# Paired transfers of edge features and receivers, and an even stream of single-row loads, in a graph-network kernel

## The chip, the cores and the metric

The kernel runs on one core of one Trainium2 chip. The metric is the device time of one execution in microseconds. Times are the median of several executions; a profile is one more execution, recorded by the hardware profiler.

## The reference

One message-passing layer over a graph of 6250 nodes and 206250 edges, sorted by receiver, followed by a residual and a layer norm. In the code below `senders` is `src`, `receivers` is `dst`, and the two feature arrays have 32 columns each; D is 128, with 8 heads of 16.

```python
w_ij = silu(edge_feats @ rad_W1 + rad_b1) @ rad_W2 + rad_b2
w_ij = w_ij + (silu(chi_scalar @ sph_W1 + sph_b1) @ sph_W2 + sph_b2)
q_i = (node_feats @ Wq)[receivers]            # by heads
k_j = (node_feats @ Wk)[senders]
alpha = (q_i * w_ij * k_j).sum(axis=-1) / sqrt(HEAD_DIM) * cutoffs[:, None]
v_j = (node_feats @ Wv)[senders]
out = segment_sum(alpha[..., None] * v_j, receivers, num_segments=n_nodes) / 16.0
x = layernorm(x + out)
```

## The kernel before

**Tiles, quads and groups.** 128 edges are a tile, four tiles a quad, and four quads a group; there are 403 quads in 101 groups (NG). The main loop goes over groups and, in each, over four slots, one quad a slot, in the order 0, 2, 1, 3. `i` counts slots.

**Before the loop** the keys and values of all nodes are computed and written to a table in DRAM, `kv_tab`, one row of 1 KB a node. The receivers of each edge, relative to the quad's first node, are turned so that a tile's 128 numbers lie in one row (`relT`), written to DRAM (`rel_lin`, L481), and copied from there four times over into `rel_four` (L486), from which a group's receivers can be read as one broadcast.

**A slot of the loop** works on several quads in different stages. TensorE runs the first layers of quad i+2 (L560), brings the queries of quad i+1 to its edges (`q_at_edges`, L579), runs the second layers of quad i+1 (`weigh`, L612), and sums the messages of the group before (L664). ScalarE applies SiLU to quad i+2 (L597). VectorE multiplies the queries of quad i+1 by its keys (`multiply`, L628), then multiplies quad i by the second layers' output (L636), reduces (L638), scales (L641) and forms the messages (L653). The last product of `q_at_edges` is the slot's mark: ScalarE's SiLU, VectorE's multiply, GpSimd's next gathers and some of SyncE's loads wait for it.

**Keys and values** come in two ways. GpSimd gathers one tile of 128 rows per instruction from `kv_tab` (L141), 14 slots ahead, four instructions a quad. For 60 of the quads, spread evenly between slots 8 and 401 (`row_at`, six or seven slots apart), the fourth tile is not gathered. Its 128 rows are fetched by 128 single DMAs of 1 KB (L214) into a tile `wide`: 60 issued from SyncE's queue (SP), 68 from ScalarE's. The row addresses are read from `at_i` into registers by loads (L208), two for SyncE's share of a tile and three for ScalarE's. `multiply` waits for a row tile's semaphore (L625).

**How the rows are dealt.** `load_rows(i)` ends each slot's code. It knows one row tile at a time. Tile k is dealt from slot `row_at[k-1] - 4` to slot `row_at[k] - 5`; in each of these slots each queue is owed an equal part of the tile's units, where a row is one unit and a load of registers is ROW_LOAD = 5. `next_rows` issues what is owed. ScalarE keeps ROW_CARRY = 2 units back, which are issued between the next slot's SiLUs. `wide` has three buffers.

**SyncE's queue** runs in program order and also issues, once a group: the node rows `x` (L315), the features of group g+3 (`load_feats`, L252, 512 KB, three buffers), the receivers of group g+3 (`load_rel`, L263, 128 KB, four buffers), and the write of finished rows (L773). The loads of `x` and of the features wait for a mark of TensorE.

Of the kernel before, what the change touches and what calls it, by code (L numbers as in the profile page):

```python
# [12 lines left out]
F32 = mybir.dt.float32  # L13
BF16 = mybir.dt.bfloat16
U8 = mybir.dt.uint8
# [6 lines left out]
SP = mybir.EngineType.SP  # L22
ACT = mybir.EngineType.Activation
WAIT = mybir.DependencyInfo(mybir.DependencyClass.Sync, mybir.DependencyReason.DATA)

P = 128
# [6 lines left out]
GT = 16  # L33
QT = 4
NQ = GT // QT
NG = math.ceil(E / (P * GT))
NT = NG * GT
EG = P * GT
EQ = P * QT
QUADS = math.ceil(E / EQ)  # L40
NB = math.ceil(N / P)
NBC = 7
ROWS = (NB + 1) * P
W = 32
LB = 4
ROW_BYTES = 2 * D * 4
# [4 lines left out]
ROW_TILES = 60  # L51
ROW_FIRST = 8
ROW_LAST = 401
ROW_LEAD = 5
ROW_ACT = 68
ROW_AT = {SP: 0, ACT: 64}
ROW_LOAD = 5
ROW_CARRY = 2
ROW_UNITS = {SP: 32, ACT: 24}
XU = 4  # L60
# [3 lines left out]
ROW_SEMS = 8  # L64
# [8 lines left out]
def gnn_kernel(ctx, tc, x, src, dst, weight, edges, rad_W1, rad_b1, rad_W2, rad_b2,  # L73
# [14 lines left out]
    nc = tc.nc  # L88
    const = ctx.enter_context(tc.tile_pool(name="const", bufs=1))
    dram = ctx.enter_context(tc.tile_pool(name="dram", bufs=1, space=DRAM))  # L90

    kv_tab = dram.tile([NB * P, 2 * D], F32, name="kv_tab")
    rel_lin = dram.tile([NT, P], BF16, name="rel_lin")
    rel_four = dram.tile([NT // QT, NQ, EQ], BF16, name="rel_four")
    acc = dram.tile([ROWS, D], F32, name="acc")

    wkv = const.tile([P, 2 * D], F32, name="wkv")
# [39 lines left out]
    def quad_of(name, bufs, width=D):  # L137
        return ep.tile([P, QT, width], F32, name=name, bufs=bufs)
# [11 lines left out]
    row_of = {}  # L150
    row_done = {}
    rows_left = {SP: [], ACT: []}
    owed = {SP: 0, ACT: 0}
    row_work = {}
    row_issued = {}
    row_sems = [tc.alloc_semaphore(f"rows_{n}") for n in range(ROW_SEMS)]
    row_count = [0] * ROW_SEMS
# [4 lines left out]
    def next_rows(engine, n, loads=True):  # L162

        left = rows_left[engine]
        n = min(n, owed[engine])
        while n > 0 and left and (loads or left[0][0] == 1):
            cost, issue = left.pop(0)
            issue()
            n -= cost
            owed[engine] -= cost  # L170
# [19 lines left out]
        kv_of[q] = kv  # L190
        kv_done[q] = kv_sems[at], kv_count[at]

    def load_rows(i):

        k = next((k for k in range(ROW_TILES) if i <= row_at[k] - ROW_LEAD), None)
        start = None if k is None else (row_at[k - 1] if k else ROW_FIRST) - ROW_LEAD + 1
        if k is None or i < start:
            return next_rows(ACT, owed[ACT])
        q = order[row_at[k]]
        slots = row_at[k] - ROW_LEAD + 1 - start  # L200
        table = kv_tab.bitcast(U8).rearrange("(o n) b -> o (n b)", o=1)

        def rows_by(engine, name, a, b):
            regs = {}

            def load(e, m):
                c = ROW_AT[name] + e - a
                regs.update(zip(range(e, e + m), nc.values_load_multi_w_load_instructions(  # L208
                    at_i[k:k + 1, c:c + m], engines=(name,), min_val=0,
                    max_val=(N - 1) * ROW_BYTES,  # L210
                    skip_runtime_bounds_check_because="senders are nodes")[1]))

            def row(p):
                signalled(engine.dma_start(row_of[q][p:p + 1, 0, :].bitcast(U8),  # L214
                                           table[:, ds(regs.pop(p), ROW_BYTES)]))

            items = []
            for e in range(a, b, ROW_UNITS[name]):
                m = min(ROW_UNITS[name], b - e)
                items.append((ROW_LOAD, lambda e=e, m=m: load(e, m)))  # L220
                items += [(1, lambda p=p: row(p)) for p in range(e, e + m)]
            rows_left[name] += items
            return sum(cost for cost, _ in items)

        def signalled(o):
            tc.no_tile_sem_insts.add(o.ins.name)
            tc.add_to_no_dep_group(f"rows_{q}", o.ins)
            o.then_inc(row_sems[k % ROW_SEMS], 16)
            row_count[k % ROW_SEMS] += 16
            row_done[q] = row_sems[k % ROW_SEMS], row_count[k % ROW_SEMS]  # L230
            row_issued[q] = row_issued.get(q, 0) + 1

        n = P - ROW_ACT
        if i == start:
            row_of[q] = quad_of("wide", 3, P)[:, :2, :].rearrange("p t d -> p (t d)")[:, None, :]
            row_work[SP] = rows_by(nc.sync, SP, 0, n)
            row_work[ACT] = rows_by(nc.scalar, ACT, n, P)
        for engine, m in row_work.items():
            a, b = (math.ceil(m * j / slots) for j in (i - start, i - start + 1))
            owed[engine] += b - a  # L240
        next_rows(SP, owed[SP])
        next_rows(ACT, owed[ACT] - ROW_CARRY)

    def kv_parts(q, t):

# [1 line left out]
            return [(t, kv_of[q][:, t, :])]  # L247
        return [(slice(0, QT - 1), kv_of[q][:, :QT - 1, :]), (slice(QT - 1, QT), row_of[q])]

    def load_feats(g, mark=None):  # L250
        feats_of[g] = gp.tile([P, EG // 2], F32, name="feats", bufs=3)
        o = nc.sync.dma_start(feats_of[g], edges[g])  # L252
        if mark is not None:
            tc.add_manual_dep(o.ins, mark.ins.name, WAIT, reason="one signal of TensorE a quad")

    def quads_in(g):
        return min(NQ, QUADS - g * NQ)

    def load_rel(g, pool, bufs):

        relb_of[g] = pool.tile([P, EQ], BF16, name="relb", bufs=bufs)
        r = rel_four[g * NQ:(g + 1) * NQ].rearrange("j n e -> (j n) e")
        nc.sync.dma_start(relb_of[g], r[:, None, :].to_broadcast([NQ * NQ, W // NQ, EQ]))  # L263

    made = []

# [72 lines left out]
    with tc.tile_pool(name="nodes", bufs=1) as nodes, \  # L339
# [134 lines left out]
            nc.tensor.transpose(pt[:n, 0, :], rel[:, t:t + n], ident)  # L474
            nc.scalar.activation(relT[:n, t // P, :], pt[:n, 0, :], AF.Copy)

        def store_rel(a, b):
            for i, n in ((slice(a, min(b, NT // P)), P), (slice(NT // P, b), NT % P)):
                if i.start < i.stop:
                    t = slice(i.start * P, i.start * P + (i.stop - i.start) * n)  # L480
                    nc.sync.dma_start(rel_lin[t, :].rearrange("(n p) e -> p n e", p=n), relT[:n, i, :])  # L481
            a, b = a * P // QT, min(b * P, NT) // QT
            r = rel_lin.rearrange("(q t) e -> q (t e)", t=QT)
            for a, b in ((a, b - b % (P // 8)), (b - b % (P // 8), b)):
                if a < b:
                    nc.sync.dma_start(rel_four[a:b], r[a:b, None, :].to_broadcast([b - a, NQ, EQ]))  # L486

        def first_rel():
            turn_rel(0)
# [29 lines left out]
        for i, (k, n) in enumerate(work):  # L519
# [20 lines left out]
            if i == len(chunks) - 1:  # L540
                load_rel(0, gp, 1)
                load_feats(0)
                for g in range(1, XL):
                    load_x(g)
                    load_feats(g)
                nc.sync.dma_start(scale, weight)
        for q in order[XQ:AHEAD]:
            gathers(q)
        nc.vector.tensor_tensor(bsum, b2[:, 0:1], b2[:, 1:2], op=OP.add)
        store_rel(1, math.ceil(NT / P))  # L550
        nc.vector.tensor_scalar(scale, scale, SCALE, None, op0=OP.mult)


    with tc.tile_pool(name="ps", bufs=1, space=PSUM) as pp, tc.tile_pool(name="loop", bufs=1) as lp:
# [241 lines left out]
            nc.vector.tensor_scalar(general, found, 0.0, None, op0=OP.is_gt)  # L796

        written, ready, ready_at = [], [], []
        load_rel(1, lp, 4)
        load_rel(2, lp, 4)  # L800
        silus(order[0], first_layers(order[0]))
        pick(1)
        q_at_edges(order[0])
# [4 lines left out]
        for g in range(NG - 1):  # L808
            for slot, j in enumerate((0, 2, 1, 3)):
# [34 lines left out]
                if slot == 0:  # L844
                    if g + XL < NG:
                        load_x(g + XL, past)
                if slot == 3 and g + 3 < NG:
                    load_feats(g + 3, past)
                if slot == 2 and g + 3 < NG:
                    load_rel(g + 3, lp, 4)  # L850
                if slot == 0 and 1 <= g:
                    one_hots(g)
                if slot == 1:
# [254 lines left out]
```

## Time and profile before

| | |
|---|---|
| median of 3 executions | 2596.52 us (2588.82 to 2597.5) |
| the profiled execution | 2599.59 us, its span 2597.7 us |
| mean granted TensorE clock | 0.837 |
| busy: PE, PEld, DVE, ACT, POOL | 2090.8, 1744.9, 1525.9, 645.0, 1470.8 us |
| gathers on GpSimd (L141) | 1520, 945 ns each |
| single rows from SyncE / from ScalarE (L214) | 3600 / 4080 |
| features, receivers (L252, L263) | 101 x 512 KB, 101 x 128 KB |

PE is TensorE's matmul, PEld its weight load, DVE is VectorE, ACT ScalarE, POOL GpSimd, SP SyncE; a q behind the name means the engine's sequencer, which waits and issues DMAs. A line of a group of instructions gives line, engine, operation, output and inputs, count, busy time, mean ns of one, then the idle time before them and what ended most of it. "Remote" stands where the profile cannot name what ended a wait. A line of the waits gives who waited for whom, microseconds in total, times, and the longest. A row of the timeline gives start, duration, instruction and count, then the idle time before it. For one line's instructions the three durations are minimum, median and maximum in ns.

### The profile page before, as it was taken

To read this page: it belongs to the slowest core of one execution; us is meant where nothing else is said; L and a number is where in the kernel's file an instruction comes from. 1 tells how busy PE (TensorE), PEld (TensorE's weight loads), DVE (VectorE), ACT (ScalarE), POOL (GpSimd) and SP (SyncE) were. 2 spreads that over 40 slices of the span, in tenths; PEclk is the share of its full clock that TensorE was granted. 3 is DMA by queue.
4 is the path that set the end of the run, shared out by engine and by line. 5 is a ranking of instruction groups with operands and counts; after the bars stand their busy time and mean duration, and the time that the engine had idled before them with its cause. 6 is when DMAs were issued, how large, how long until landed. Compare 5 with 4: busy or idle time off the path is not lost.

```text
span 2597.7 us, 56700 instructions
## 1 busy us (share of the span) xinstructions
PE 2090.8 (80%) x15990; PEld 1744.9 (67%) x15990; DVE 1525.9 (59%) x3427; ACT 645.0 (25%) x1359; POOL 1470.8 (57%) x1564
## 2 busy tenths in 40 slices
PE   5678888888888788878888878888887888888787
PEld 4567677666767666666667667666766767676666
DVE  3456556656656555656656556555656556565567
ACT  1122222222222222222222222222222222222223
POOL 4456565655565565555556555555555555565540
PEclk7788888888888888888888797888788787887888
DMA  5543444434343343434434434444343343443331
GB/s 180 173 118 112 120 124 116 121 112 122 113 123 116 116 124 114 120 112 122 121 111 123 119 114 121 115 120 121 114 120 118 111 122 115 119 124 108 118 103 35
DMA packets 157219, 307.18 MB, mean 118 GB/s; under 512 B 42022, under 2 KB 91360, under 8 KB 156896
## 3 DMA queue, kind: packets, MB, share of 16 engines
q0 software_dynamic: 73984, 201.43, 27.2%
q1 hardware_dynamic: 72976, 97.35, 11.4%
q10 hardware_dynamic: 9936, 4.72, 0.8%
q8 instruction: 127, 2.08, 0.3%
q14 instruction: 196, 1.61, 0.2%
HBM read 289.88 MB, written 15.11 MB: 117 GB/s over the span
## 4 chain that ended last, share of the span: by engine, by line
PE 38%; issue 20%; SPq 13%; DVE 13%; another core or an unknown queue 10%; ACTq 5%; ACT 1%; DMA 0%; DVEq 0%
PE pw L612 17%; SPq L214 10%; PE pq L579 7%; PE ph L560 6%; ACTq L214 4%; PE po L664 3%; DVE kq L628 3%; DVE side L638 2%; DVE kq L636 2%; SPq L208 2%; PE pq L705 1%; ACT act L597 1%; PE pk L381 1%; PE pq L286 1%
## 5 line engine op out<-in xcount | busy, mean ns | idle before, releaser
L141 POOL DMA_INDIRECT kv<-kv_tab,src_i x1520 | 1436.9, 945 | 1042.9 <-remote 447.9
L612 PE MATMUL pw<-w,act 128*128 128x128 f32 x6448 | 1060.4, 324 | 109.1 <-issue 107.6
L612 PEld LDWEIGHTS pw<-w,act 128*128 128x128 f32 x6448 | 951.7, 231 | 187.0 <-issue 149.7
L597 ACT ACTIVATE act<-ph,b 128x512 f32<-128x512 f32 x806 | 554.7, 689 | 1843.5 <-remote 1374.7
L628 DVE TENSOR_TENSOR kq<-pq,kv 128x512 f32<-128x512 f32 (+1 forms) x404 | 270.6, 670 | 931.3 <-remote 680.0
L560 PE MATMUL ph<-feats,w 32*128 32x512 f32 x1612 | 665.7, 740 | 138.5 <-issue 128.8
L579 PE MATMUL pq<-q,hotT 32*128 32x128 f32 x3224 | 557.5, 321 | 20.9 <-issue 17.8
L579 PEld LDWEIGHTS pq<-q,hotT 32*128 32x128 f32 x3224 | 470.7, 220 | 33.0 <-issue 32.7
L560 PEld LDWEIGHTS ph<-feats,w 32*128 32x128 f32 x1612 | 190.7, 207 | 303.6 <-issue 272.0
L638 DVE TENSOR_REDUCE side<-kq 128x32 f32<-128x512 f32 x404 | 280.2, 694 | 14.0
L653 DVE TENSOR_TENSOR msg<-kv,side 128x512 f32<-128x512 f32 (+1 forms) x404 | 268.7, 665 | 13.9
L636 DVE TENSOR_TENSOR kq<-pw,kq 128x512 f32<-128x512 f32 x404 | 274.1, 679 | 0.0
L664 PE MATMUL po<-msg,hot 128*32 128x128 f32 x3200 | 183.2, 309 | 34.2 <-issue 34.1
L567 PE MATMUL pw<-brow,onesb 3*128 3x512 bf16 x403 | 176.5, 438 | 0.0
L664 PEld LDWEIGHTS po<-msg,hot 128*32 128x32 f32 x3200 | 84.5, 118 | 91.2 <-issue 63.6
L705 PE MATMUL pq<-part,to 128*128 128x128 f32 x196 | 56.6, 380 | 107.6 <-issue 54.4
L705 PEld LDWEIGHTS pq<-part,to 128*128 128x128 f32 x196 | 38.6, 245 | 122.2 <-issue 83.7
L641 DVE TENSOR_TENSOR side<-side,scale 128x32 f32<-128x32 f32 x400 | 79.7, 199 | 13.7
L381 PE MATMUL pk<-wkv,xT 128*128 128x256 f32 x162 | 45.6, 424 | 38.0 <-DVE kv L382 23.9
L292 DVE TENSOR_TENSOR hotT<-relb,side 128x512 f32<-128x512 bf16 x101 | 68.6, 679 | 0.0
L286 PE MATMUL pq<-wq,xT 128*128 128x128 f32 x200 | 49.6, 336 | 23.5 <-issue 15.9
L382 DVE COPY kv<-pk 128x512 f32<-128x512 f32 (+1 forms) x41 | 27.4, 682 | 68.9 <-remote 48.5
(126 smaller groups left out, 892.9 us busy)
## 6 DMA issues: line engine op xcount, KB each, us to landing
wide<-kv_tab ACTq DMA_DIRECT2D x4080, 1.0 KB
wide<-kv_tab SPq DMA_DIRECT2D x3600, 1.0 KB
feats<-in_edges SPq DMA_DIRECT2D x101, 512.0 KB
kv<-kv_tab,src_i POOLq DMA_INDIRECT x1520, 2.9
relb<-rel_four SPq DMA_DIRECT2D x101, 128.0 KB
x<-in_x SPq DMA_DIRECT2D x101, 64.0 KB
out<-y SPq DMA_DIRECT2D x101, 64.0 KB
kv_tab<-kv SPq DMA_DIRECT2D x12, 512.0 KB
```

The lines of the kernel that those rows point to most:

```text
L141: return nc.gpsimd.indirect_dma_start(out=o, out_offset=None, in_=table, in_offset=bass.IndirectOffsetOnAxis(ap=index, axis=0))
L214: signalled(engine.dma_start(row_of[q][p:p + 1, 0, :].bitcast(U8), table[:, ds(regs.pop(p), ROW_BYTES)]))
L560: return nc.tensor.matmul(act_of[q, i], w1[r0:r0 + R, :], feats_of[g][r0:r0 + R, c0:c0 + EQ], start=True, stop=True)
L567: nc.tensor.matmul(pw, onesb[f:f + 3, :], brow[f:f + 3].rearrange("p t d -> p (t d)"), start=True, stop=False)
L579: o = nc.tensor.matmul(pq_of[q][:, t, :], hotT_of[g][b, t * P:(t + 1) * P], q_of[g][b, :], start=True, stop=True)
L597: o = nc.scalar.activation(act, act_of[q, i], AF.Silu, bias=b1[:, i:i + 1])
L612: o = nc.tensor.matmul(pw[:, t, :], act_of[q, i][:, t * P:(t + 1) * P], w2[:, i, :], start=False, stop=(t == QT - 1 and i == 1))
L628: o = nc.vector.tensor_tensor(kq_of[q][:, u, :], pq_of[q][:, u, :], kv[:, :, :D], op=OP.mult)
L636: nc.vector.tensor_tensor(m, pw_of[q][:, t, :], m, op=OP.mult)
L638: nc.vector.tensor_reduce(alpha, m.rearrange("p t (h e) -> p t h e", e=HD), AX.X, OP.add)
L653: nc.vector.tensor_tensor(msg_of[q][:, u, :].rearrange("p t (h e) -> p t h e", e=HD), kv[:, :, D:].rearrange("p t (h e) -> p t h e", e=HD) ...
L664: o = nc.tensor.matmul(po_of[g][j * W:(j + 1) * W, :], hot_of[g][:, j * QT + t, :], msg_of[g * NQ + j][:, t, :], start=(t == 0), stop=(t = ...
```

## The change

Features and receivers are loaded for two groups at a time: `load_feats` and `load_rel` take a pair u (groups 2u and 2u+1), are called in the odd groups only, and keep two buffers of double size each. For this the receivers lie in DRAM by pairs (`rel_pair`), and `store_rel` writes them with more and smaller DMAs: ten writes and six broadcasts in all, where there were three and three. The row tiles are no longer dealt one at a time. `load_rows(i)` works out how many tiles are due by slot i as one number, 60/393 of a tile a slot; it opens each tile as this number passes it, and owes each queue the units between the last slot's number and this one's. A load of registers now counts six units, and the lead is six slots.

```diff
--- before.py
+++ after.py
@@ -38,6 +38,7 @@
 EG = P * GT
 EQ = P * QT
 QUADS = math.ceil(E / EQ)
+PAIRS = math.ceil(NG / 2)
 NB = math.ceil(N / P)
 NBC = 7
 ROWS = (NB + 1) * P
@@ -51,10 +52,10 @@
 ROW_TILES = 60
 ROW_FIRST = 8
 ROW_LAST = 401
-ROW_LEAD = 5
+ROW_LEAD = 6
 ROW_ACT = 68
 ROW_AT = {SP: 0, ACT: 64}
-ROW_LOAD = 5
+ROW_LOAD = 6
 ROW_CARRY = 2
 ROW_UNITS = {SP: 32, ACT: 24}
 XU = 4
@@ -90,8 +91,8 @@
     dram = ctx.enter_context(tc.tile_pool(name="dram", bufs=1, space=DRAM))
 
     kv_tab = dram.tile([NB * P, 2 * D], F32, name="kv_tab")
-    rel_lin = dram.tile([NT, P], BF16, name="rel_lin")
-    rel_four = dram.tile([NT // QT, NQ, EQ], BF16, name="rel_four")
+    rel_lin = dram.tile([2, PAIRS, GT, P], BF16, name="rel_lin")
+    rel_pair = dram.tile([PAIRS, NQ, NQ, 2, EQ], BF16, name="rel_pair")
     acc = dram.tile([ROWS, D], F32, name="acc")
 
     wkv = const.tile([P, 2 * D], F32, name="wkv")
@@ -151,7 +152,8 @@
     row_done = {}
     rows_left = {SP: [], ACT: []}
     owed = {SP: 0, ACT: 0}
-    row_work = {}
+    row_dealt = {SP: 0, ACT: 0}
+    row_open = []
     row_issued = {}
     row_sems = [tc.alloc_semaphore(f"rows_{n}") for n in range(ROW_SEMS)]
     row_count = [0] * ROW_SEMS
@@ -190,15 +192,11 @@
         kv_of[q] = kv
         kv_done[q] = kv_sems[at], kv_count[at]
 
-    def load_rows(i):
-
-        k = next((k for k in range(ROW_TILES) if i <= row_at[k] - ROW_LEAD), None)
-        start = None if k is None else (row_at[k - 1] if k else ROW_FIRST) - ROW_LEAD + 1
-        if k is None or i < start:
-            return next_rows(ACT, owed[ACT])
+    def open_tile(k):
+
         q = order[row_at[k]]
-        slots = row_at[k] - ROW_LEAD + 1 - start
         table = kv_tab.bitcast(U8).rearrange("(o n) b -> o (n b)", o=1)
+        row_of[q] = quad_of("wide", 3, P)[:, :2, :].rearrange("p t d -> p (t d)")[:, None, :]
 
         def rows_by(engine, name, a, b):
             regs = {}
@@ -211,8 +209,14 @@
                     skip_runtime_bounds_check_because="senders are nodes")[1]))
 
             def row(p):
-                signalled(engine.dma_start(row_of[q][p:p + 1, 0, :].bitcast(U8),
-                                           table[:, ds(regs.pop(p), ROW_BYTES)]))
+                o = engine.dma_start(row_of[q][p:p + 1, 0, :].bitcast(U8),
+                                     table[:, ds(regs.pop(p), ROW_BYTES)])
+                tc.no_tile_sem_insts.add(o.ins.name)
+                tc.add_to_no_dep_group(f"rows_{q}", o.ins)
+                o.then_inc(row_sems[k % ROW_SEMS], 16)
+                row_count[k % ROW_SEMS] += 16
+                row_done[q] = row_sems[k % ROW_SEMS], row_count[k % ROW_SEMS]
+                row_issued[q] = row_issued.get(q, 0) + 1
 
             items = []
             for e in range(a, b, ROW_UNITS[name]):
@@ -222,24 +226,20 @@
             rows_left[name] += items
             return sum(cost for cost, _ in items)
 
-        def signalled(o):
-            tc.no_tile_sem_insts.add(o.ins.name)
-            tc.add_to_no_dep_group(f"rows_{q}", o.ins)
-            o.then_inc(row_sems[k % ROW_SEMS], 16)
-            row_count[k % ROW_SEMS] += 16
-            row_done[q] = row_sems[k % ROW_SEMS], row_count[k % ROW_SEMS]
-            row_issued[q] = row_issued.get(q, 0) + 1
-
         n = P - ROW_ACT
-        if i == start:
-            row_of[q] = quad_of("wide", 3, P)[:, :2, :].rearrange("p t d -> p (t d)")[:, None, :]
-            row_work[SP] = rows_by(nc.sync, SP, 0, n)
-            row_work[ACT] = rows_by(nc.scalar, ACT, n, P)
-        for engine, m in row_work.items():
-            a, b = (math.ceil(m * j / slots) for j in (i - start, i - start + 1))
-            owed[engine] += b - a
+        row_open.append({SP: rows_by(nc.sync, SP, 0, n), ACT: rows_by(nc.scalar, ACT, n, P)})
+
+    def load_rows(i):
+
+        tiles = min(max((i - ROW_FIRST + ROW_LEAD) * ROW_TILES / (ROW_LAST - ROW_FIRST), 0), ROW_TILES)
+        while len(row_open) < math.ceil(tiles):
+            open_tile(len(row_open))
+        for engine in owed:
+            due = sum(min(max(tiles - k, 0), 1) * work[engine] for k, work in enumerate(row_open))
+            owed[engine] += math.ceil(due) - row_dealt[engine]
+            row_dealt[engine] = math.ceil(due)
         next_rows(SP, owed[SP])
-        next_rows(ACT, owed[ACT] - ROW_CARRY)
+        next_rows(ACT, owed[ACT] - (ROW_CARRY if tiles < ROW_TILES else 0))
 
     def kv_parts(q, t):
 
@@ -247,20 +247,31 @@
             return [(t, kv_of[q][:, t, :])]
         return [(slice(0, QT - 1), kv_of[q][:, :QT - 1, :]), (slice(QT - 1, QT), row_of[q])]
 
-    def load_feats(g, mark=None):
-        feats_of[g] = gp.tile([P, EG // 2], F32, name="feats", bufs=3)
-        o = nc.sync.dma_start(feats_of[g], edges[g])
+    def pair_of(u):
+        return range(2 * u, min(2 * u + 2, NG))
+
+    def load_feats(u, mark=None):
+        pair = pair_of(u)
+        feats = gp.tile([P, 2, EG // 2], F32, name="feats")
+        for g in pair:
+            feats_of[g] = feats[:, g - pair[0], :]
+        o = nc.sync.dma_start(feats[:, :len(pair), :],
+                              edges[pair[0]:pair[-1] + 1].rearrange("g p e -> p g e"))
         if mark is not None:
             tc.add_manual_dep(o.ins, mark.ins.name, WAIT, reason="one signal of TensorE a quad")
 
     def quads_in(g):
         return min(NQ, QUADS - g * NQ)
 
-    def load_rel(g, pool, bufs):
-
-        relb_of[g] = pool.tile([P, EQ], BF16, name="relb", bufs=bufs)
-        r = rel_four[g * NQ:(g + 1) * NQ].rearrange("j n e -> (j n) e")
-        nc.sync.dma_start(relb_of[g], r[:, None, :].to_broadcast([NQ * NQ, W // NQ, EQ]))
+    def load_rel(u, pool, bufs):
+
+        pair = pair_of(u)
+        n = len(pair) * EQ
+        relb = pool.tile([P, 2 * EQ], BF16, name="relb", bufs=bufs)
+        for g in pair:
+            relb_of[g] = relb[:, (g - pair[0]) * EQ:(g - pair[0] + 1) * EQ]
+        r = rel_pair[u].rearrange("j n h e -> (j n) (h e)")[:, :n]
+        nc.sync.dma_start(relb[:, :n], r[:, None, :].to_broadcast([NQ * NQ, W // NQ, n]))
 
     made = []
 
@@ -474,16 +485,23 @@
             nc.tensor.transpose(pt[:n, 0, :], rel[:, t:t + n], ident)
             nc.scalar.activation(relT[:n, t // P, :], pt[:n, 0, :], AF.Copy)
 
-        def store_rel(a, b):
-            for i, n in ((slice(a, min(b, NT // P)), P), (slice(NT // P, b), NT % P)):
-                if i.start < i.stop:
-                    t = slice(i.start * P, i.start * P + (i.stop - i.start) * n)
-                    nc.sync.dma_start(rel_lin[t, :].rearrange("(n p) e -> p n e", p=n), relT[:n, i, :])
-            a, b = a * P // QT, min(b * P, NT) // QT
-            r = rel_lin.rearrange("(q t) e -> q (t e)", t=QT)
-            for a, b in ((a, b - b % (P // 8)), (b - b % (P // 8), b)):
-                if a < b:
-                    nc.sync.dma_start(rel_four[a:b], r[a:b, None, :].to_broadcast([b - a, NQ, EQ]))
+        def store_rel(c, d):
+
+            ends_at = [min(d, (NG + 1 - h) // 2) for h in range(2)]
+            for u in range(c, min(c + NQ, d)):
+                for h, e in enumerate(ends_at):
+                    p, n = u % NQ * 2 * GT + h * GT, len(range(u, e, NQ))
+                    nc.sync.dma_start(
+                        rel_lin[h, u:e:NQ].rearrange("n m e -> m n e"),
+                        relT[p:p + GT, u // NQ:u // NQ + n, :])
+            for h, e in enumerate(ends_at):
+                r = rel_lin[h].rearrange("u (j t) e -> (u j) (t e)", t=QT)
+                m = e - (e - c) % NQ
+                for x, y in ((c, m), (m, e)):
+                    if x < y:
+                        nc.sync.dma_start(
+                            rel_pair[x:y, :, :, h, :].rearrange("u j n e -> (u j) n e"),
+                            r[x * NQ:y * NQ, None, :].to_broadcast([(y - x) * NQ, NQ, EQ]))
 
         def first_rel():
             turn_rel(0)
@@ -542,12 +560,12 @@
                 load_feats(0)
                 for g in range(1, XL):
                     load_x(g)
-                    load_feats(g)
+                load_feats(1)
                 nc.sync.dma_start(scale, weight)
         for q in order[XQ:AHEAD]:
             gathers(q)
         nc.vector.tensor_tensor(bsum, b2[:, 0:1], b2[:, 1:2], op=OP.add)
-        store_rel(1, math.ceil(NT / P))
+        store_rel(1, PAIRS)
         nc.vector.tensor_scalar(scale, scale, SCALE, None, op0=OP.mult)
 
 
@@ -796,8 +814,7 @@
             nc.vector.tensor_scalar(general, found, 0.0, None, op0=OP.is_gt)
 
         written, ready, ready_at = [], [], []
-        load_rel(1, lp, 4)
-        load_rel(2, lp, 4)
+        load_rel(1, lp, 2)
         silus(order[0], first_layers(order[0]))
         pick(1)
         q_at_edges(order[0])
@@ -844,10 +861,10 @@
                 if slot == 0:
                     if g + XL < NG:
                         load_x(g + XL, past)
-                if slot == 3 and g + 3 < NG:
-                    load_feats(g + 3, past)
-                if slot == 2 and g + 3 < NG:
-                    load_rel(g + 3, lp, 4)
+                if slot == 3 and g % 2 == 1 and g + 3 < NG:
+                    load_feats((g + 3) // 2, past)
+                if slot == 2 and g % 2 == 1 and g + 3 < NG:
+                    load_rel((g + 3) // 2, lp, 2)
                 if slot == 0 and 1 <= g:
                     one_hots(g)
                 if slot == 1:
```

## The prediction

> **What bounds the kernel now.** I read the page first, then the waits, then two stretches of the loop against each other.
>
> ```profile
> span 2597.7 us, 56700 instructions
> ...
> q10 hardware_dynamic: 9936, 4.72, 0.8%
> ...
> L141 POOL DMA_INDIRECT kv<-kv_tab,src_i x1520 | 1436.9, 945 | 1042.9 <-remote 447.9
> ...
> POOL kv L141 <- remote: 447.9, 292, 2.2
> POOL kv L141 <- issue: 352.0, 1130, 3.7
> ```
>
> The loop handles one quad of edges a slot. GpSimd issues four gathers in an ordinary slot and three in a slot whose later quad gets its fourth tile by single rows. One gather takes 0.945 us, the gap to the next one 352.0/1130 = 0.31, and the wait that opens a slot 447.9/292 = 1.53. So a slot of four is 4 x 0.945 + 3 x 0.31 + 1.53 = 6.24 us, and a slot of three 4.98. A row tile falls on every 6.55th slot (393 slots, 60 tiles), which makes 6.05 us a slot on average, if GpSimd alone sets the pace. The counts of the DVE product that runs once a slot say when it does:
>
> ```profile
> core 0: us, DVE busy (x), PEclk, DMA share, GB/s
> 206.00:644.00 438.00, 48.96 (x72) 0.86 0.40 118
> 723.00:2433.00 1710.00, 186.97 (x275) 0.84 0.40 117
> ```
>
> Early it is 438/72 = 6.083 us a slot, later 1710/275 = 6.218. The difference, 0.135 us a slot, is what this change can win. The waits of the later stretch, and the whole loop's waits of SyncE's queue, say where it comes from:
>
> ```profile
> DVE kq L628 <- DVEq L625: 41.6, 10, 6.4
> DVE kq L628 <- DMA wide<-kv_tab: 36.7, 7, 6.6
> ...
> SPq L773 <- ACT act L597: 1.7, 4, 0.5
> ```
>
> VectorE waits for single rows, 78 us in 17 named waits (L625 is the wait for a row tile's semaphore), and SyncE's queue, which issues 60 of a tile's 128 rows, waits for no one: its longest entry between 330 and 2500 us is 1.7 us. It is simply full. The timeline shows how it came to be late. The first two rows below end one tile's share and are followed by its multiply; then the same at 722 us and at 886 us.
>
> ```profile
> 290.16 10.10 SPq L214 DMA_DIRECT2D wide<-kv_tab  x20
> 300.29 0.53 SPq L263 DMA_DIRECT2D relb<-rel_four  x1
> 327.98 0.56 DVE L628 TENSOR_TENSOR kq<-pq,kv 128x384 f32<-128x384 f32 x1 [1.50 <-remote]
> ...
> 712.89 6.05 SPq L214 DMA_DIRECT2D wide<-kv_tab  x11
> 722.77 0.56 DVE L628 TENSOR_TENSOR kq<-pq,kv 128x384 f32<-128x384 f32 x1 [0.97 <-remote]
> ...
> 878.70 6.16 SPq L214 DMA_DIRECT2D wide<-kv_tab  x11
> 886.49 0.56 DVE L628 TENSOR_TENSOR kq<-pq,kv 128x384 f32<-128x384 f32 x1 [4.05 <-DVEq L625]
> ```
>
> At slot 34 the last row is issued 327.98 - 300.26 = 27.7 us ahead. At slot 99 it is 722.77 - 718.94 = 3.8 us, and at slot 125 only 1.6 us, and VectorE idles 4.05 us. So SyncE loses 23.9 us in 65 slots, 0.37 a slot, and from about slot 99 on its lateness is paid in the loop. The queue is the second bound, and from there on the binding one.
>
> **The change, part by part.** What SyncE issues in an unpaid stretch (330 to 640 us), and the issues themselves:
>
> ```profile
> wide<-kv_tab SPq DMA_DIRECT2D x438, 1.0 KB
> feats<-in_edges SPq DMA_DIRECT2D x12, 512.0 KB
> relb<-rel_four SPq DMA_DIRECT2D x12, 128.0 KB
> ...
> L252 SPq DMA_DIRECT2D feats<-in_edges x101: 3/359/757, 71.4 to 2549.4; - x101
> L252 SPq EVENT_SEMAPHORE  x97: 3/17/716, 158.7 to 2549.3; - x97
> L263 SPq DMA_DIRECT2D relb<-rel_four x101: 3/539/912, 70.5 to 2544.6; - x101
> L315 SPq DMA_DIRECT2D x<-in_x x101: 3/356/793, 57.9 to 2536.8; - x101
> ```
>
> *Pairs of features and receivers.* Every eight slots one feature issue with its semaphore wait (0.359 + 0.017) and one receiver issue (0.539) go. With a gap of some 0.05 us for each of the three, as between 300.26 and 300.29, that is about 1.0 us less on SyncE's queue per eight slots. What is left may cost more. Bytes do not set an issue's time: 64 KB take 0.356 and 512 KB take 0.359. The number of steps in its pattern may: receivers, read with a broadcast step, take 0.18 more. The pair of features gets such a step (partition, group, element), and receivers have it already. So I take 1.0 - 0.18 = 0.82 us saved per eight slots, 0.10 a slot. The ends are 1.0 (no growth) and 0 (the new issue takes what two took; nothing in these rows suggests more than that).
>
> The data itself is covered. The first group of a pair is still loaded seven slots, 43 us, before its use; SyncE's lag of 27.7 - 1.6 = 26 us leaves 17. A load of 512 KB fills the DMA engines for one or two microseconds:
>
> ```profile
> 334.42 0.37 SPq L252 DMA_DIRECT2D feats<-in_edges  x1
> 336.00:337.00 1.00, 1.00 (x8) 0.84 (x8) 0.93 (x3) 0.10 (x1) 0.70 (x2) 0.66 0.95 355
> ```
>
> At 355 GB/s 1 MB needs about 3 us, well inside 17. Uncovered, it would hold up the first layers by what is missing. Rows issued behind it may land later. The Trainium skill ("DMA: Bandwidth & Descriptors", Queues, rings and completion order) says that each DMA engine consumes its descriptors in ring order. By that rule a tile is hit if its last rows follow the burst within some 3 us of each 50 (8 slots), once in 16 tiles, for at most 3 us: 43 tiles x 3/50 x 3 = 8 us at most, against half of that already paid for the single bursts; I leave it out of the sum.
>
> *The even stream.* Tiles are due six or seven slots apart (27 and 33 times). Before, SyncE's 70 units were dealt over exactly those slots, 11.7 or 10 a slot; now 72 units (a load of registers counts six) flow at 11.0. A queue that is behind takes its work in order whatever the dealing, and the due slots are unchanged, so evenness as such gains nothing on SyncE. The code order moves: the last call that still deals a tile stays five slots ahead for 57 of 60 tiles, but now holds the rest of that tile and the start of the next, so its last row is on average half a slot, 3 us, earlier (0 to 6.1). This is added once to the lead.
>
> *ScalarE's share* of 68 rows and three loads goes from 83 units over six or seven slots (13.8 or 11.9) to 86 at an even 13.1. It moves work between slots and takes none away; its price is a rival below, and zero in the sum.
>
> *Before the loop.* The receiver store grows from three writes and three broadcasts to ten and six. Most lie here:
>
> ```profile
> 109.51 1.09 SPq L481 DMA_DIRECT2D rel_lin<-relT  x2
> 112.42 1.47 SPq L486 DMA_DIRECT2D rel_four<-rel_lin  x2
> 114.01 1.22 SPq L263 DMA_DIRECT2D relb<-rel_four  x2
> 123.62 0.38 SPq L315 DMA_DIRECT2D x<-in_x  x1
> 137.52 0.35 SPq L315 DMA_DIRECT2D x<-in_x  x1
> ```
>
> Six more writes at 0.55 and two more broadcasts at 0.74 are 4.8 us, and the load of the second pair must now wait for the broadcast to land. SyncE stands still from 115.2 to 123.6 and again before 137.5 for TensorE's marks, so this is hidden; without that cover it would be some 5 to 9 us. Receivers of groups 0 and 1 come from the early, separate store; group 2 is needed only at the fifth slot.
>
> *The sum.* Saving 0.10 a slot, SyncE loses 0.27 instead of 0.37. Its lead, 23.9 + 3, then lasts 100 slots instead of 65, so lateness is paid from slot 134, not 99. I scale its price with the shortfall: 0.135 x 0.27/0.37 = 0.099 us a slot. Up to the last tile at slot 394: before 295 x 0.135 = 39.8, after 260 x 0.099 = 25.7, a gain of 14 us. With 1.0 saved: shortfall 0.245, from slot 144, 250 x 0.089 = 22.3, gain 17.5. With nothing saved: the 3 us of lead alone, 1 us. The profiled execution took 2599.6 us, 1.9 of them outside its span, and the median of the runs is 2596.5; the difference of 14 carries over: **2582.5 us**.
>
> **The rivals.** The bound for a change that a measurement here can tell is 0.3%, 7.8 us.
>
> *Full cover (0.13).* The 0.37 is an average with large swings; SyncE issues faster while GpSimd idles. If the saved time suffices to keep up, the later stretch runs at 6.083 like the early one: 39.8 us less, 2556.5. Against it: 0.10 to 0.125 is a third of the shortfall.
>
> *No change (0.20).* The doubled transfer may take two issues' time, or the freed time may go into slower rows. Then only the lead is left, 1 us: 2595.5. The same skill page (Issuing engines are not separate DMA queues) calls the sequencer's time to initiate a DMA usually small relative to the DMA itself; by that rule fewer issues save nothing, 2596.5. The trace disagrees: a row costs 6.16/11 = 0.56 us of SyncE, while the packets of ScalarE's queue, nearly all such rows, took 0.8% x 16 x 2597.7/9936 = 0.03 us each.
>
> *Slower: ScalarE becomes late (0.20).* Its queue holds the rows in front of the next slot's SiLU, and that is already tight:
>
> ```profile
> 2404.36 5.60 ACTq L214 DMA_DIRECT2D wide<-kv_tab  x11
> 2410.01 0.69 ACT L597 ACTIVATE act<-ph,b 128x512 f32<-128x512 f32 x1 [4.98 <-remote]
> ```
>
> Eleven rows take 5.60 us, 0.51 each, and end 0.05 us before the SiLU. Behind the rows stand the SiLUs, and behind these TensorE's next products. In the 33 seven-slot tiles 1.3 units more come in a slot, 0.65 us; in the three slots without a register load that is up to 33 x 3 x 0.65 = 64 us. The 27 six-slot tiles get 0.7 units, 0.36 us, back: 27 x 3 x 0.36 = 29. Net 35, less the 14: 2617.5 at worst, and slower from the point where half of it reaches the path. For it: no spare time in that slot. Against it: the heaviest slots become lighter, and ScalarE's lateness must first outlast the wait for TensorE's mark.
>
> **How the numbers follow.** The forecast has 0.47, with a range of its own from 2575 to 2595.5. Faster by over 0.3% are full cover, 0.13, and all but 0.02 of the forecast: 0.58. Within 0.3% lie 0.02 + 0.20 = 0.22; slower 0.20. The range runs from the full cover's 2556 to 2606, which takes in the first three cases and the nearer part of the last.
>
> **What the changed profile would show.** Right: 51 feature issues of 1024 KB and 51 receiver issues of 256 KB at about 0.55 us each; the waits of L628's product for rows still there but fewer, starting some 30 slots later; 6.15 to 6.19 us a slot in the late stretch, 6.08 early. Wrong: issues of about 1 us; early slots longer than 6.1, with SiLUs starting after ScalarE's rows and not after TensorE's mark; VectorE or TensorE waiting for features or receivers; or a late stretch still at 6.22.

## The result, and the profile after

The changed kernel takes 2567.64 us (median of 5 executions, 2562.14 to 2575.41) against 2596.71 for the kernel before, run beside it (5 executions, 2588.82 to 2599.69). The ratio is 0.9893 [0.9869, 0.9918]: 29 us or 1.1% faster. The forecast was 14 us faster, 2582.5; the time lies inside the range, the size is off by a factor of two. The profiled execution took 2568.07 us at a granted clock of 0.840 (before 0.837). One thing has to be known to read what follows: on the three chips on which the experiments ran, the kernel before takes 1973 to 1975 us, not 2597; what differs in the traces is told with them, and its cause is open.

The pairs do what they say. From the page of the changed kernel, the span and the issues of SyncE's queue, and then the durations (minimum, median, maximum in ns) of the two lines that load pairs and of the waits ahead of them:

```profile
span 2566.2 us, 56501 instructions
...
feats<-in_edges SPq DMA_DIRECT2D x50, 1024.0 KB
...
relb<-rel_pair SPq DMA_DIRECT2D x50, 256.0 KB
```

```profile
L258 SPq DMA_DIRECT2D feats<-in_edges x51: 3/402/694, 70.2 to 2520.0; - x51
L258 SPq EVENT_SEMAPHORE  x3: 13/17/626, 257.2 to 355.7; - x3
...
L274 SPq DMA_DIRECT2D relb<-rel_pair x51: 3/540/1074, 69.1 to 2515.7; - x51
```

A feature issue moves twice the bytes and grows from 0.359 to 0.402 us; a receiver issue stays at 0.54. Half of the issues are gone, and with them 94 of the 97 semaphore waits in front of the features.

The pace of the loop, by the product that runs once a slot (columns as in the prediction; it is L654 now):

```profile
core 0: us, DVE busy (x), PEclk, DMA share, GB/s
206.00:644.00 438.00, 48.95 (x72) 0.86 0.41 120
723.00:2433.00 1710.00, 189.63 (x279) 0.84 0.40 119
```

The early stretch holds 72 slots as before. The late one holds 279 instead of 275: 1710/279 = 6.129 us a slot, where it was 6.218. VectorE's waits for single rows in that stretch, and then the largest entry of SyncE's queue between 330 and 2460 us:

```profile
DVE kq L646 <- DVEq L643: 36.8, 8, 9.8
DVE kq L646 <- DMA wide<-kv_tab: 27.5, 5, 6.8
```

```profile
SPq L274 <- DVE kq L654: 1.2, 3, 0.6
```

64 us in 13 waits, before 78 in 17, and SyncE still waits for no one. Its queue is still full, only less late. The timeline shows by how much, at the multiplies of slots 34, 99, 125 and 171, each behind the last row of its tile where that row stands out; the last line is slot 197:

```profile
317.86 8.21 SPq L212 DMA_DIRECT2D wide<-kv_tab  x16
...
325.41 0.56 DVE L646 TENSOR_TENSOR kq<-pq,kv 128x384 f32<-128x384 f32 x1 [1.26 <-remote]
...
695.17 4.50 SPq L212 DMA_DIRECT2D wide<-kv_tab  x7
...
717.12 0.56 DVE L646 TENSOR_TENSOR kq<-pq,kv 128x384 f32<-128x384 f32 x1 [1.04 <-remote]
...
875.20 0.56 DVE L646 TENSOR_TENSOR kq<-pq,kv 128x384 f32<-128x384 f32 x1
...
1145.65 2.90 SPq L212 DMA_DIRECT2D wide<-kv_tab  x8
...
1150.68 0.56 DVE L646 TENSOR_TENSOR kq<-pq,kv 128x384 f32<-128x384 f32 x1 [0.96 <-PE pq L597]
...
1316.59 0.56 DVE L646 TENSOR_TENSOR kq<-pq,kv 128x384 f32<-128x384 f32 x1 [9.80 <-DVEq L643]
```

At slot 99 the tile's last row is issued by 699.67, 717.12 - 699.67 = 17.4 us ahead; before it was 3.8. At slot 125 the multiply follows its neighbours without a wait, where it idled 4.05 us before. At slot 171 the lead is down to 1150.68 - 1148.55 = 2.1 us, and at slot 197 VectorE waits 9.80 us. By tiles, the lead falls from 32.8 us at slot 34 to 3.3 at slot 158: 29.5/124 = 0.24 us a slot, where it was 0.37. (In a run of rows that ends inside a tile, as at 317.86, the last row is found by counting rows.)

Where the 31.5 us of the two spans come from shows in the time at which the same multiply runs in both traces. First before, then after, at slots 86, 184 and 401 (slots 99 and 125 stand above and in the prediction). Slot 184 is the first row tile at which the changed kernel's multiply waits several microseconds for rows:

```profile
643.89 0.56 DVE L628 TENSOR_TENSOR kq<-pq,kv 128x384 f32<-128x384 f32 x1 [1.43 <-PE pq L579]
...
1251.08 0.56 DVE L628 TENSOR_TENSOR kq<-pq,kv 128x384 f32<-128x384 f32 x1 [5.15 <-DMA wide<-kv_tab]
...
2577.90 0.55 DVE L628 TENSOR_TENSOR kq<-pq,kv 128x384 f32<-128x384 f32 x1
```

```profile
639.10 0.56 DVE L646 TENSOR_TENSOR kq<-pq,kv 128x384 f32<-128x384 f32 x1 [1.23 <-PE pq L597]
...
1232.04 0.56 DVE L646 TENSOR_TENSOR kq<-pq,kv 128x384 f32<-128x384 f32 x1 [4.22 <-DMA wide<-kv_tab]
...
2547.16 0.55 DVE L646 TENSOR_TENSOR kq<-pq,kv 128x384 f32<-128x384 f32 x1
```

The changed kernel is 4.8 us ahead at slot 86, 5.65 at slot 99, 19.0 at slot 184 and 30.7 at slot 401.

| stretch | gain measured | gain by the prediction's steps |
|---|---|---|
| to slot 99, nobody late yet | 5.7 us | 0 |
| slots 99 to 184, late before, in time after | 13.4 us (0.16 a slot) | 4.7 us (35 slots x 0.135) |
| slot 184 to the end, both late | 11.7 us (0.05 a slot) | 9.4 us (260 slots x 0.036) |

### The profile page after: what moved, and what is told of

The parts are those of the page before. It is cut to its first block, busy times and chain, and to the rows that moved or that the text cites. A ratio compares the mean times of both kernels' runs of the same rounds, so it can differ in the third digit from the quotient of the medians.

```text
span 2566.2 us, 56501 instructions
## 1 busy us (share of the span) xinstructions
PE 2081.7 (81%) x15990; PEld 1736.8 (68%) x15990; DVE 1525.9 (59%) x3427; ACT 641.3 (25%) x1359; POOL 1470.3 (57%) x1564
## 3 DMA queue, kind: packets, MB, share of 16 engines
q10 hardware_dynamic: 9936, 4.72, 0.8%
## 5 line engine op out<-in xcount | busy, mean ns | idle before, releaser
L654 DVE TENSOR_TENSOR kq<-pw,kq 128x512 f32<-128x512 f32 x404 | 274.1, 678 | 0.0
L682 PE MATMUL po<-msg,hot 128*32 128x128 f32 x3200 | 185.2, 313 | 33.1 <-issue 32.7
L308 DVE TENSOR_TENSOR hot<-rel,side 128x512 f32<-128x512 f32 x100 | 67.9, 679 | 0.0
```

The costliest lines, as they stand in the source:

```text
L654: nc.vector.tensor_tensor(m, pw_of[q][:, t, :], m, op=OP.mult)
L682: o = nc.tensor.matmul(po_of[g][j * W:(j + 1) * W, :], hot_of[g][:, j * QT + t, :], msg_of[g * NQ + j][:, t, :], start=(t == 0), stop=(t = ...
```

## Experiments

Three theories were on record. **Q**: the gain is SyncE's queue, which has some hundred issues less. **S**: it is the even stream, which relieves ScalarE's queue, whose rows stand in front of the SiLU. **R**: the time freed on SyncE goes into slower rows, so that little or nothing is left. To take the change apart, the experiments use one program text in which the dealing is chosen for each queue by itself; with both switches off or both on, and the matching loads, it issues what the two kernels issue.

### The parts alone

```diff
-ROW_LEAD = 6
-ROW_LOAD = 6
+EVEN = {SP: 0, ACT: 0}          # e1: paired loads, rows dealt tile by tile
+ROW_LEAD = {SP: 5, ACT: 5}
+ROW_LOAD = {SP: 5, ACT: 5}
...
+EVEN = {SP: 1, ACT: 1}          # e2: loads by groups as before, both queues even
+EVEN = {SP: 0, ACT: 1}          # e3: the same, ScalarE's rows alone even
+EVEN = {SP: 1, ACT: 0}          # e4: the same, SyncE's rows alone even
```

A queue that is even has ROW_LEAD and ROW_LOAD 6, the other 5.

> The kernel before with the paired transfers alone; the rows are dealt tile by tile as before. Theory Q (the whole gain of 29 us is SyncE's queue, which has 50 feature and 50 receiver issues less): nearly all of the gain is here, 2570 to 2575 us, and ScalarE's SiLUs still start late in about 55 slots, 41 us in all, as before. Theory S (the even stream relieves ScalarE's queue, and this gives half or more): about 2582 us.

> The kernel before with the even stream of rows alone; features and receivers are loaded group by group as before. Theory Q: at most the half slot of lead, 2594 to 2597 us. Theory S: about 2582 us, with the SiLUs late in some 12 slots and 15 us in all, as in the changed kernel.

> The kernel before with ScalarE's rows alone dealt as an even stream (lead six, a load counted six); SyncE's rows tile by tile, single loads. Theory Q: 2597 us, no change. Theory S: most of what the even stream gives as a whole, about 2583 us.

> The kernel before with SyncE's rows alone dealt as an even stream; ScalarE's rows tile by tile, single loads. Theory Q: 2594 to 2596 us, the half slot of lead. Theory S: 2595 us, the same small lead; ScalarE's SiLUs as late as before.

Measured, with the kernel before at 1973.13 us on the same chip: e1 1974.93 us, ratio 1.0011 [1.0002, 1.0020]; e2 1970.21, 0.9987 [0.9977, 0.9996]; e3 1971.42, 0.9993 [0.9984, 1.0002]; e4 1970.96, 0.9991 [0.9982, 1.0000]. The expectations counted on 2597 us; that the kernel before would run in 1973 us was foreseen by none of them, and all four expected some 2570 to 2600 us. No part's ratio lies more than 0.13% from 1 here, in either direction. So the next runs had to ask what is different on these chips.

### Both kernels whole on such a chip, and the share of ScalarE

```diff
 # e5: the changed kernel; e6: the kernel before
-ROW_ACT = 68
+ROW_ACT = 64                    # e7: the changed kernel, 64 rows from each queue
...
-ROW_ACT = 68
+ROW_ACT = 72                    # e8: the changed kernel, 56 from SyncE, 72 from ScalarE
-ROW_AT = {SP: 0, ACT: 64}
+ROW_AT = {SP: 0, ACT: 60}
```

> The changed kernel itself, beside the kernel before. In the runs of the prediction TensorE's mark reached the other engines 2.4 us after the modelled end of its matmul, and SyncE needed 0.57 us a row; in the first four experiments it was 0.05 us and 0.33 us, the kernel before took 1973 us, and SyncE's rows lay 14 us and more ahead. Theory Q (the gain is SyncE's queue): where marks are prompt SyncE binds nothing, so within 0.3% of before; where marks are late again, 1% faster. Theory S (an even ScalarE queue): about 1968 us with prompt marks.

> The kernel before itself, for a trace from this chip. Both theories: with prompt marks SyncE's last rows lie 14 us or more ahead of their multiply and ScalarE's SiLUs start some 1.6 us after the mark; with late marks the reverse, SyncE 2 us ahead and SiLUs on time.

> The changed kernel with 64 of a tile's rows on SyncE and 64 on ScalarE, instead of 60 and 68. This takes 4 rows of 0.32 us, 1.3 us a tile, from ScalarE and gives them to SyncE. Theory Q, late marks: SyncE gets 60 x 4 x 0.56 = 134 us of work more, its lateness starts near the first tiles: 15 to 40 us slower than the changed kernel. Theory Q, prompt marks: ScalarE binds there, so 20 to 60 us faster. Theory S: faster in both cases.

> The changed kernel with 56 of a tile's rows on SyncE and 72 on ScalarE. Theory Q, late marks: SyncE no longer falls behind, 10 to 25 us faster than the changed kernel, unless ScalarE becomes late. Theory Q, prompt marks: 20 to 60 us slower. Theory S: slower in both cases.

The changed kernel took 1976.48 us against 1974.15, 1.0008 [0.9999, 1.0017]: no difference. The kernel before, traced, took 1973.07. Its windows of the once-a-slot product, its timeline in one slot, and its chain of waits by engine:

```profile
300.00:1900.00 1600.00, 229.74 (x339) 0.94 0.54 153
```

```profile
1001.78 3.45 ACTq L214 DMA_DIRECT2D wide<-kv_tab  x10
...
1003.04 0.60 PE L579 MATMUL pq<-q,hotT 32*128 32x128 f32 x4
...
1003.72 0.69 DVE L628 TENSOR_TENSOR kq<-pq,kv 128x512 f32<-128x512 f32 x1 [0.49 <-PE pq L579]
...
1005.28 0.69 ACT L597 ACTIVATE act<-ph,b 128x512 f32<-128x512 f32 x1 [2.84 <-issue]
```

```profile
ACTq 37%; DMA 20%; issue 14%; PE 10%; DVE 8%; POOL 7%; ACT 5%; DVEq 0%; POOLq 0%
```

A slot takes 1600/339 = 4.72 us. The multiply starts 0.08 us after the mark's matmuls end (1003.04 + 0.60). The SiLU that waits for the same mark starts 1.56 us later, behind ten rows that ScalarE's sequencer issues from 1001.78 to 1005.23. In the trace behind the prediction it is the other way round; the same two instructions there:

```profile
2405.67 0.60 PE L579 MATMUL pq<-q,hotT 32*128 32x128 f32 x4
...
2407.59 0.95 POOL L141 DMA_INDIRECT kv<-kv_tab,src_i  x1 [0.30 <-issue]
...
2409.97 0.69 DVE L628 TENSOR_TENSOR kq<-pq,kv 128x512 f32<-128x512 f32 x1 [2.61 <-remote]
```

There the multiply starts 2409.97 - 2406.27 = 3.70 us after the matmuls end. By the mark's own semaphore the signal comes 2.69 us after the modelled end there, in the median of the loop (2.84 in the changed kernel's trace), and 0.05 here. So here the marks are prompt, the slot is shorter, and the largest part of the chain goes through ScalarE's queue; SyncE's has no share in it. SyncE is also quicker: its median from row to row is 0.32 us, against 0.565, and its last rows come 14 us or more ahead all along.

The chain does not name what holds the time. The largest wait of GpSimd's gathers does, between 300 and 1900 us of the same trace (e6):

```profile
POOL kv L141 <- issue: 329.6, 1080, 0.3
```

No gather waits more than 0.3 us. In each of the eight traces e1 to e8 the 1520 gathers run from 44 to 47 us until 1945 to 1949 us, and no gap between two of them is over 0.33 us. GpSimd is full, whatever is changed elsewhere, and only the 21 to 43 us behind the last gather can differ. In the kernel before of the prediction the gathers did wait, 447.9 us for what opens a slot. So e1 to e5 agree with theory Q, since SyncE does not bind here, but they cannot tell it from S: with GpSimd as the bound, neither could show a gain.

e7 took 1978.68 us, 1.0027 [1.0015, 1.0040], where Q expected 20 to 60 us less from moving four rows a tile off ScalarE: a miss. Its chain, and that of e8 (1997.54 us, 1.0123 [1.0107, 1.0138]):

```profile
ACTq 23%; DMA 20%; PE 17%; SPq 16%; DVE 10%; issue 10%; ACT 3%; DVEq 0%; POOL 0%; POOLq 0%
```

```profile
ACTq 59%; issue 14%; PE 12%; ACT 7%; DVE 5%; DMA 1%; SPq 0%; DVEq 0%
```

With 64 rows each, SyncE's queue enters the chain with 16%; with 72 on ScalarE that queue has 59% of it. In both the gathers end as in e6, at 1946.7 and 1947.0 us against 1947.1. What differs is the time behind them: 24.2 us in e6, 32.7 in e5, 30.2 in e7 and 42.7 in e8. So Q's expectation for e7 failed because it took ScalarE's queue for the bound, and the bound was GpSimd. For e8 it expected 20 to 60 us more than the changed kernel; against e5 it is 21.1 us more.

### SyncE made to bind

The condition of the prediction's trace did not come back, so the last four runs brought about the one part of it that theory Q needs: SyncE's queue as the bound. Of a tile's 128 rows 88 go to SyncE and 40 to ScalarE.

```diff
-ROW_ACT = 68
+ROW_ACT = 40
-ROW_AT = {SP: 0, ACT: 64}
+ROW_AT = {SP: 0, ACT: 88}
 # o1: with the kernel before; o2: the changed kernel; o3: pairs alone (as e1); o4: even stream alone (as e2)
```

> The kernel before with 88 of a tile's rows on SyncE and 40 on ScalarE, so that SyncE's queue is the bound also where marks are prompt; the base of the three that follow. All theories: a tile's share on SyncE costs about 88 x 0.37 + 3 x 2.1 + 4 us = 43 us against 30 us of slots, so about 2550 to 2750 us, and SyncE's last row is issued about 2 us ahead of its multiply.

> The changed kernel with the same 88 and 40 rows. Theory Q (removed issues on a binding queue): per pair of groups 2 x 0.45 for features and 2 x 0.60 for receivers go and 0.46 + 0.61 come, 0.9 to 1.0 us, 50 times: 45 to 50 us less than o1_before, and some 3 us for the lead. Theory R (SyncE's freed time goes into slower rows, and the pairs are worth nothing by themselves): within 5 us of o1_before. Theory S (the even stream helps through ScalarE): within 5 us, since ScalarE with 40 rows has time to spare.

> The paired transfers alone, with 88 and 40 rows, dealt tile by tile. Theory Q: 45 to 50 us less than o1_before, nearly as o2_after. Theories R and S: within 5 us of o1_before.

> The even stream alone, with 88 and 40 rows, single loads. Theory Q: the half slot of lead alone, 0 to 6 us less than o1_before. Theories R and S: the same. If it gives 20 us or more, the dealing matters on SyncE itself, against the reasoning that a queue which is behind does not care how its work is dealt.

Measured: o1 2469.93 us (2467.73 to 2471.03; ratio to the kernel before 1.2510 [1.2493, 1.2528]), o2 2414.27 (1.2230 [1.2213, 1.2247]), o3 2413.93 (1.2224 [1.2207, 1.2241]), o4 2468.78 (1.2503 [1.2482, 1.2523]). The pairs are worth 56.0 us, the even stream 1.2 (within the scatter of o4's runs, 2464.86 to 2472.15), both together 55.7. The base was expected at 2550 to 2750 us, too slow; Q expected 45 to 50 us of the pairs and 3 more in o2, somewhat too little. In o1, SyncE's largest wait between 200 and 2400 us is 1.6 us in total, and the gathers have 456 us of gaps over 0.5 us, so SyncE is full there and GpSimd is not. VectorE's wait for the semaphore of single rows, first in o1, then in o2:

```profile
DVE kq L645 <- DVEq L642: 777.1, 59, 16.8
```

```profile
DVE kq L664 <- DVEq L661: 721.5, 59, 17.2
```

It is 55.6 us shorter, all of the gain. What SyncE issues between 600 and 2000 us, in o1 and in o3:

```profile
wide<-kv_tab SPq DMA_DIRECT2D x3118, 1.0 KB
feats<-in_edges SPq DMA_DIRECT2D x58, 512.0 KB
relb<-rel_four SPq DMA_DIRECT2D x57, 128.0 KB
```

```profile
wide<-kv_tab SPq DMA_DIRECT2D x3190, 1.0 KB
feats<-in_edges SPq DMA_DIRECT2D x30, 1024.0 KB
relb<-rel_pair SPq DMA_DIRECT2D x30, 256.0 KB
```

55 issues of features and receivers fewer make room for 72 rows more, 2.3% more rows in the same time; 56.0/2470 is 2.3% as well. This is the mechanism of Q, shown for prompt marks: on a queue that is full, an issue that is dropped gives its time to the rows behind it. Per pair of groups it is 56.0/50 = 1.12 us. R is refuted here: a row takes 0.335 us of SyncE in o1 and 0.333 in o3, on average. S as the whole of the gain is refuted for these runs, and o4 shows that the dealing does not matter to a SyncE queue that is late; what it does for ScalarE is not tested here, as ScalarE has 40 rows instead of 68. And the rule of the Trainium skill ("DMA: Bandwidth & Descriptors", Issuing engines are not separate DMA queues) that the sequencer's time to initiate a DMA is usually small relative to the DMA itself does not hold here: by it o1 and o3 would be equal, as they move the same bytes.

Under the late marks of the prediction R holds in part. From slot 171 to slot 374, where the queue is late in both traces, SyncE issues the same 1860 rows, but a row takes 0.553 us of it after the change and 0.535 before. That is 34 us more, while its issues of features and receivers take 18 us less; all else that it issues and waits for takes some 24 us less, so the stretch is only 8.3 us shorter (1263.2 to 1254.9 us). What slows the rows was not tested. Over the loop the median from row to row, before the change, is 0.68 us while the gathers run and 0.32 in their pauses.

## Why the prediction was right, point by point

**The bound and the mechanism: right.** SyncE's queue never waits, loses its lead slot by slot, and is paid for in the loop once the lead is gone. The changed trace shows the same decline, slower, and the o runs show that dropped issues alone bring a gain when that queue binds. The e runs show the other side: where GpSimd binds and SyncE has slack, the same edit is worth nothing. The two lengths of a slot are right too: from slot 2 to slot 84 of the kernel before, slots with four gathers take 6.29 us and slots with three 4.78 on average, where 6.24 and 4.98 were worked out. But GpSimd does not set them alone: the 1.53 us that the sum counts with its gathers are a wait for TensorE's mark. Under late marks this mark follows the gathers: of 385 marks (slots 3 to 387) half come 1.19 to 1.37 us after the end of the slot's last gather, and 5 come while a gather runs; in e6 181 of 385 do. No instruction makes the mark wait for these gathers, whose rows are multiplied some 80 us later. So in the late condition the slot is the gathers and then the mark, one after the other.

**The saving by pairs: mis-sized.** The step took 1.0 us less 0.18 for a longer pattern, 0.82 per eight slots. The feature issue grew by 0.04 us, not 0.18, and the receiver issue not at all. So the upper end of that step, 1.0, was the right value. The fall of the lead agrees: 0.37 - 0.24 = 0.13 us a slot, 1.04 per eight slots. The o runs give 1.12, on chips with prompt marks. What was wrong in it is the row by which the growth was sized: receivers with a broadcast step take 0.18 us more than a plain load, but that is no price for a third step in a pattern.

**The lead from the even stream: right in kind.** At the first four row tiles (slots 14 to 34) the lead is 2.3, 5.3, 2.1 and 5.1 us longer than before, where 3 (0 to 6.1) was expected. Part of it can be the pairs', which save from the start. That the dealing itself gains nothing on a late SyncE queue is shown by o4, for prompt marks.

**Onset and price of lateness: onset too early, price about right.** With more saved and more lead, lateness is paid from about slot 184, not 134; this is a larger miss in the sum than the price. The stretch in which only the kernel before is late returned 0.16 us a slot, near the 0.135 that is the difference of 6.218 and 6.083. From there on the gain is 0.05 us a slot, where scaling with the shortfall gave 0.036, and would give 0.135 - 0.135 x 0.24/0.37 = 0.047 with the shortfall that was measured. The scaling had no mechanism behind it, and that it came out is partly luck: a full queue that saves 0.13 us a slot should return 0.13, and the slower rows told above took most of the difference. (The sum also ends at slot 394, where the last row tile is at 401; that is worth under 1 us.) The late stretch came out at 6.129 us a slot, a little below the 6.15 to 6.19 that were named as right.

**What is not settled.** How the 29 us divide between the pairs and the even stream was not measured under late marks. With the onset and the shortfall that were measured, the prediction's working gives 85 x 0.135 + 217 x 0.047 = 21.7 us of the 30.7 between the traces. The largest part that it lacks is the 5.7 us gained before slot 99: 1.8 us ahead of the first row tile, whose multiply runs at 204.27 us instead of 206.05, and 3.9 between slots 14 and 99. A candidate for the latter is ScalarE's queue. Its waits in which nothing but its own issuing held the SiLU, over the whole run, before and then after:

```profile
ACT act L597 <- issue: 42.4, 12, 5.2
```

```profile
ACT act L615 <- issue: 20.3, 8, 4.0
```

They halve. SiLUs that start over 0.15 us after their mark's semaphore were 54 and are 12, and their lateness falls from 35 to 15 us; between slots 14 and 99 it falls by 4.0 us, from 7.8 to 3.8. An even deal of ScalarE's rows would do this, but under late marks it was not tried by itself, as the condition did not come back, and where marks were prompt (e3, 0.9993) GpSimd's gathers were the bound. It stays an argument.

**The rivals.** *Slower by ScalarE* did not come: fewer SiLUs were late than before, not more. What a row costs in front of the SiLU under late marks was not measured; e8 ran with prompt marks. *No change* came true on the chips with prompt marks, for a reason that the rival did not name: GpSimd's gathers are the bound there. The second half of that rival, freed time that goes into slower rows, came true in part, as told above. *Full cover* did not come: VectorE still waits 64 us for rows in the late stretch. The longer prologue cost nothing, as said: the first row tile's multiply runs 1.8 us earlier. Bursts of 1 MB left no trace in the waits for rows in flight, 27.5 us in 5 where they were 36.7 in 7; no run measured them alone.

## What to carry to other kernels

When a DMA queue never waits and the lead of its transfers shrinks from tile to tile, count its issues and not its bytes: merging two issues gives the time of one to whatever stands behind, wholly in the o runs, and less where the rows behind became slower. Before counting on it, find out whether that queue ends the wait in the stretch in question, since the same edit was worth 1% where it did and nothing where GpSimd ran without a gap. And before an experiment, look for the engine that is full in it: behind such an engine, no theory about another queue can show. And when the lead is long, the gain is set by when it runs out, so size the rate of loss and not only the saving.

## What the runs showed of the hardware that was not expected

The same program runs in 2597 us and in 1973 us. In the long runs TensorE's mark reaches the other engines 2.69 us (median) after the modelled end of its matmul, against 0.05; SyncE goes from row to row in 0.565 us, against 0.32; the granted clock is 0.837, against 0.943 to 0.956; a gather takes 945 ns in the one trace and 947 in the other. The experiments' three chips all showed the short time, and the executions on which the result rests all the long one. A low granted clock by itself does not make the marks late: in o1 it is 0.821, and the mark comes after 0.06 us. Both delays go with the gathers: in the long trace marks come behind them, and SyncE's rows take 0.68 us while they run and 0.32 in their pauses; with prompt marks it is 0.32 us either way (o1). ScalarE's rows show no such split, 0.318 us in both. Whether the gathers themselves hold up TensorE's signal and SyncE's rows, and why in some executions alone, is open.

An issue's time hardly depends on the bytes it moves: 64 KB took 0.356 us, 512 KB 0.359 and 1 MB 0.402, and two receivers' broadcasts in one issue took 0.540 us, one 0.539.
